# Reordering the opening and the first hand-over of a two-layer adjacency kernel

## The chip, the cores and the metric

One core of one Trainium2 chip runs the whole kernel. The metric is the device time of one execution in microseconds, as a median of runs. The engines are named as in the profile: PE (matrix multiply), PEld (its weight loads), DVE (vector), ACT (activations), POOL and SP (which here mostly issues DMAs).

## The reference: two graph layers on sixteen graphs

For each of 16 graphs, `x` is 1024 x 128 and `adj` is 1024 x 1024 of zeros and ones, all float32. Layer 0 is an attention with gates, layer 1 has four heads (cut to what matters):

```python
h  = x @ Ww.T + Wb
e  = (h @ A) @ h.T ;  e = e + e.T
att = softmax(where(adj > 0, e, 0), axis=1) * adj
hp = relu(att @ h)
ic, fc, oc = (sigmoid(hp @ w_u + x @ w_x) for each gate)
x  = layernorm(x + oc * tanh(ic * hp + fc * x))
# layer 1, per head
h1 = x @ conv_w[hd] + conv_b[hd]
Ah = tanh(adj * (h1 @ attn_w[hd] @ h1.T))
x  = layernorm(x + relu(relu(mean_hd(relu(Ah @ h1))) + x))
```

## The kernel before: tiles, stages and the order of the work

A graph is cut into eight blocks of 128 rows (`NB`), or two halves of 512 columns. The kernel is a software pipeline over graphs: while layer 1 of graph b runs (32 steps of one head and one block, `layer1_step`, lines 589 to 622), pieces of layer 0 of graph b+1 are put between its matmuls. Every engine executes its own instructions strictly in the order in which the program issues them, and that order is written by hand: `run(first, "...")` takes named pieces of layer 0 of graph 0, `run(second, "...")` those of graph 1. For graph 0 there is no layer 1 to hide behind, so lines 674 to 716 order the opening alone.

The pieces have one-letter names: `L` loads a block of adj, `E` makes a 0/1 mask of it (line 383), `Q` projects a half of `qT` (line 242), `H`/`h` multiply and add a third of `h` (lines 327, 331), `S` is a block row of scores: a matmul at line 346 and an ACT eviction at line 349 into the big tile `R`. Scores are symmetric, so only the upper triangle is multiplied. `T` transposes the rest: for graph 0 on PE (line 364) with an ACT copy (line 365), for later graphs through DRAM (`hop`, lines 263 to 276). `A` masks a block row in place and takes its maximum on DVE (line 390), then ACT takes the exponential (line 397). `B` multiplies by adj on DVE (line 406), scales a block of `h` on ACT (line 411) and accumulates the block before on PE (line 422). `R` and `P` give hp and its transpose (lines 431, 441, 442), `G` the gates and `u = fc * x` on POOL (lines 466 to 478), `I` adds `ic * hp` and takes tanh (lines 504, 508), `O`, `V`, `N` end in the layer norm (lines 515, 217 to 222, 233). After that `turn_first_x1` transposes the new x (lines 569, 570), `head_uT` multiplies it by a head's weights (line 242, `pT_u`) and layer 1 of graph 0 can start.

Ahead of this the weights are prepared (lines 66 to 164): `a_sym = A + A.T`, `s_ww = a_sym @ Ww` (`p_s`), `q_w = Ww.T @ s_ww` (`p_q`), bias vectors (`p_c`, `p_sb`, `p_bsb`), the rows of the three gates and of Wb turned to columns (`p_rows`). `keep_at_work` (line 136) issues transposes of the identity whose results nobody reads. `join_weights` (line 176) joins the layer-1 weights in four parts, each `next(join)` one of them: `p_last`; `cw` on DVE and `p_cwT`; `p_caT`; `p_m`.

PSUM has four tiles of 128 x 512 (tag `sc`) for everything but the accumulators. A matmul into one waits until the instruction that read its former content is done.

Of the kernel before, what the change touches and what calls it, by code (L numbers as in the profile page):

```python
# [19 lines left out]
P = 128  # L20
# [4 lines left out]
def two_layer_adjacency_kernel(  # L25
# [37 lines left out]


    ident = consts.tile([P, P], F32, name="ident")
    make_identity(nc, ident)
# [8 lines left out]

    rows_x = sb.tile([4, P], F32, tag="s1", name="rows_x", bufs=4)
    for g, w in enumerate((Wb, wi_x, wf_x, wo_x)):
        nc.scalar.dma_start(rows_x[g : g + 1], w.rearrange("(o d) -> o d", o=1))
    rows_u = sb.tile([3, P], F32, tag="turn", name="rows_u", bufs=2)
    for g, w in enumerate((wi_u, wf_u, wo_u)):  # L80
        nc.gpsimd.dma_start(rows_u[g : g + 1], w.rearrange("(o d) -> o d", o=1))

# [15 lines left out]

    def load_late_weights():
        nc.sync.dma_start(cw_in[0:1], conv_b.rearrange("(o h) d -> o h d", o=1))  # L100
        nc.sync.dma_start(cw_in[1:P], conv_w[:, 0 : D - 1, :].rearrange("h f d -> f h d"))
        nc.sync.dma_start(cw_last, conv_w[:, D - 1 : D, :].rearrange("h f d -> f h d"))
        nc.sync.dma_start(aw, attn_w.rearrange("h i j -> i h j"))
        for g, w in enumerate((wi_u, wf_u, wo_u)):
            nc.sync.dma_start(wu_b[:, g, :], w.partition_broadcast(P))
# [20 lines left out]
    q_w = consts.tile([P, P], F32, name="q_w")  # L126
    c_col = consts.tile([P, 1], F32, name="c_col")
    sb_col = consts.tile([P, 1], F32, name="sb_col")
    b_wide = sb.tile([P, P], F32, tag="uT1", name="b_wide")
    ones = sb.tile([1, P], F32, tag="u", name="ones", bufs=1)  # L130
    nc.gpsimd.memset(ones, 1.0)

# [3 lines left out]
    def keep_at_work(n):  # L136
        for _ in range(n):
            nc.tensor.transpose(idle[:, :P], ident, ident)

    keep_at_work(8)  # L140
    pa, pb = small("p_a"), small("p_ww")
    nc.tensor.transpose(pa[:, :P], a_in, ident)
    nc.tensor.transpose(pb[:, :P], ww_in, ident)
    nc.vector.tensor_add(a_sym, pa[:, :P], a_in)
    nc.scalar.copy(wwT, pb[:, :P])
    keep_at_work(2)
    pa, pb = small("p_s"), small("p_rows")
    nc.tensor.matmul(pa[:, :P], a_sym, ww_in, start=True, stop=True)
    nc.vector.tensor_copy(s_ww, pa[:, :P])
    nc.tensor.matmul(pb[:, :4], rows_x, ident[:4, :4], start=True, stop=True)  # L150
    nc.tensor.matmul(pb[:, P : 2 * P], ones, rows_x[0:1, :], start=True, stop=True)
    nc.vector.tensor_copy(wb_col, pb[:, 0:1])
    nc.vector.tensor_copy(gate_x, pb[:, 1:4])
    nc.scalar.copy(wb_row[:, :D], pb[:, P : 2 * P])
    nc.gpsimd.tensor_copy(b_wide, wb_col.to_broadcast([P, P]))
    pa, pc = small("p_q"), small("p_c")
    nc.tensor.matmul(pa[:, :P], s_ww, ww_in, start=True, stop=True)
    nc.vector.tensor_copy(q_w, pa[:, :P])
    nc.tensor.matmul(pc[:, :1], s_ww, wb_col, start=True, stop=True)
    nc.vector.tensor_copy(c_col, pc[:, :1])  # L160
    nc.vector.tensor_copy(wwT_g[:, G - 1 : G], pc[:, :1])
    pd = small("p_sb")
    nc.tensor.matmul(pd[:, :1], a_sym, wb_col, start=True, stop=True)
    nc.vector.tensor_copy(sb_col, pd[:, :1])

    def finish_weights():
        pt = small("p_bsb")
        nc.tensor.matmul(pt[:, :1], b_wide, sb_col, start=True, stop=True)
        nc.vector.tensor_copy(wb_row[:, G - 1 : G], pt[:, :1])

    def turn_rows_u():
# [119 lines left out]
    def layer0(b):  # L291
# [22 lines left out]
        def project_q(q):  # L314
            if q == 0:
                t["qT"] = sb.tile([P, N], F32, tag="qT0", name=f"qT0_{b}", bufs=1)
            project_T(t["qT"], q_w, t["xT"], c_col, f"q0_{b}", [q])

# [19 lines left out]

        def score(j):
            if j == 0:  # L340

                t["R"] = sb.tile([P, NB, NB, P], F32, tag="R", name=f"R_{b}", bufs=1)
            for q in range(j // BH, NH):
                ps = ps_sc.tile([P, 512], F32, tag="sc", name=f"sc0_{b}_{j}_{q}")
                lo, at = max(q * 512, j * P), (q + 1) * 512
                nc.tensor.matmul(  # L346
                    ps[:, : at - lo], t["qT"][:, ts(j, P)], t["xT"][:, lo:at], start=True, stop=True
                )
                nc.scalar.activation(  # L349
                    t["R"][:, lo // P : at // P, j, :],  # L350
                    ps[:, : at - lo].rearrange("p (k d) -> p k d", d=P),
                    AF.Identity, bias=t["h"][:, j, G - 1 : G],
                )

        def turn_score(j):
# [3 lines left out]
            if b == 0:  # L359
                for l0 in range(0, L, 4):  # L360
                    ls = range(j + 1 + l0, min(j + 5 + l0, NB))
# [12 lines left out]
            hop(R[:, j, j + 1 :, :], sq[:, :w], f"turn0_{b}_{j}")  # L374

        def find_edges(j):

            if b == 0:
                m = sb.tile([P, N], BF16, tag="h1", name=f"edge_{b}_{j}", bufs=NB + 1)
            else:  # L380
                m = sb.tile([P, N], U8, tag="edge", name=f"edge_{b}_{j}")
            engine = nc.vector if b == 0 and j not in (1, 4, 6) else nc.gpsimd
            engine.tensor_scalar(m, adj_t[b, j], 0.0, None, ALU.is_gt)  # L383
# [86 lines left out]
        def forget():  # L470
            t["u"] = sb.tile([P, NB, D], F32, tag="u", name=f"u0_{b}", bufs=1)
            t["x1"] = sb.tile([P, NB, D + 1], F32, tag="x1", name=f"x1_{b}")
            for ks in PARTS:
                nc.gpsimd.tensor_mul(
                    t["u"][:, ks], t["x"][:, ks],
                    t["gate"][:, ks, 1:2].to_broadcast([P, ks.stop - ks.start, D]),
                )
            nc.gpsimd.memset(t["x1"][:, :, 0:1], 1.0)
# [51 lines left out]
        if b == 0:  # L530
            pieces.update(P=lambda: rows_hp(GROUPS), G=gates)
        else:
# [11 lines left out]
        for j in range(NB):  # L544
# [4 lines left out]
            if j + 1 < NB:  # L549
                pieces[f"T{j}"] = partial(turn_score, j)  # L550
        return pieces

# [124 lines left out]
    run(second, "L0 L1 L2 L3 L4 L5 L6 L7")  # L677
    run(first, "E0 E1 E4 E6 Q0")
    finish_weights()
    run(first, "H0 h0 E2 S0 Q1 T0 S1 A0 E3 T1 S2 A1 H1 h1 B0 T2 S3 A2 E5 B1 H2 h2 T3 S4 A3 E7 B2")  # L680
    turn_rows_u()
# [3 lines left out]
    run(second, "H0")  # L685
    run(first, "B6 B7")
    run(second, "h0")
    run(first, "R")
    run(second, "H1 h1")
    run(first, "P")  # L690
    run(second, "H2 h2")
    next(join)
    run(first, "G")
    run(second, "S0")
    run(first, "I0")
    next(join)
    run(first, "I1")
    run(second, "S1")
    next(join)
    run(first, "O0 V0 O1")  # L700
    run(second, "S2")
    next(join, None)
    run(first, "N0")
    run(second, "S3")
    turn_first_x1(x1_t[0], 0)
# [7 lines left out]
    land()  # L713
    run(second, "T2 E0 Q1")
    rows(0, range(BH, NB))
# [105 lines left out]
```

## Time and profile before

| | us |
|---|---|
| median of 4 runs | 2421.18 (2420.8 to 2421.99) |
| the profiled execution | 2421.18 |
| its span in the profile | 2419.4 |
| PE busy | 2404.4 (99% of the span) |
| DVE busy | 1553.2 (64%) |
| ACT busy | 1074.2 (44%) |
| POOL busy | 613.6 (25%) |

The span is the time from the first to the last instruction of the profile; the rest of the execution's time, 1.78 us, lies around it. Times in rows are microseconds from the start of the span, durations too unless marked ns. In a row of a timeline the first number is the start, the second the duration, then engine, line, operation, what it writes and reads, and how many instructions are merged in the row. In the chain of waits each row is a start, a duration, and the work that carried the chain then.

### The profile page before, as it was taken

The page shows a single profiled execution, that of the slowest core. Times are in us where ns is not written, and L with a number is a line of the kernel's source. Part 1 is how long each engine was busy: PE and PEld are TensorE (multiplying, and loading weights), DVE is VectorE, ACT ScalarE, POOL GpSimd, SP SyncE. Part 2 cuts the span into 40 slices and gives each one's busy share as a digit, 9 for nine tenths or more (in the row PEclk, how much of TensorE's full clock was granted, in tenths as well). Part 3 has the DMA queues.
Part 4 walks back from the last instruction along what each step waited for, and adds up shares of the span by engine and source line. Part 5 has one row for each costly group of instructions (what it writes and reads, how often), then busy time and mean ns, then how long its engine had stood idle before and what let it go on. Part 6 is the DMA issues. An engine that isn't in the chain of part 4 may idle for free.

```text
span 2419.4 us, 20189 instructions
## 1 busy us (share of the span) xinstructions
PE 2404.4 (99%) x5966; PEld 1097.7 (45%) x5966; DVE 1553.2 (64%) x3274; ACT 1074.2 (44%) x1502; POOL 613.6 (25%) x382
## 2 busy tenths in 40 slices
PE   8999999999999999999999999999999999999998
PEld 5444444444444444444444444444444444444444
DVE  6656576666666666676666665666666576666554
ACT  5544444443444544444444454444544344443333
POOL 2314031241312413124131331312214132141000
PEclk9999999999999999999999999999999999999999
DMA  4334151341514415143242432425234252341010
GB/s 179 79 69 114 44 136 48 83 126 34 139 37 95 114 48 126 44 104 96 57 118 52 111 81 66 109 61 122 61 72 112 53 127 56 79 117 31 18 26 9
DMA packets 473308, 196.71 MB, mean 81 GB/s; under 512 B 414442, under 2 KB 439278, under 8 KB 473199
## 3 DMA queue, kind: packets, MB, share of 16 engines
q1 hardware_dynamic: 454519, 128.70, 22.5%
q0 software_dynamic: 18384, 66.59, 9.1%
q8 instruction: 47, 0.77, 0.1%
q14 instruction: 62, 0.51, 0.1%
q10 hardware_dynamic: 296, 0.13, 0.0%
HBM read 135.86 MB, written 59.51 MB: 81 GB/s over the span
## 4 chain that ended last, share of the span: by engine, by line
PE 98%; DVE 1%; ACT 0%; DMA 0%; issue 0%; POOL 0%; POOLq 0%; DVEq 0%; ACTq 0%
PE sc L606 36%; PE acc L612 36%; PE acc L422 9%; PE sc L346 5%; PE pR L577 5%; PE pT_u L242 5%; PE pR_h L327 1%; PE pT_q L242 1%; DVE R L390 0%; DVE R L406 0%; PE acc_q L635 0%; DMA a_in<-in_L_gnn_A_dram 0%; DMA rows_x<-in_L_gnn_wo_x_dram 0%; ACT R L397 0%; PE pt L441 0%
## 5 line engine op out<-in xcount | busy, mean ns | idle before, releaser
L607 DVE TENSOR_TENSOR s<-sc,adj 128x512 f32<-128x512 f32 x1008 | 685.4, 688 | 715.8 <-PE sc L606 694.7
L608 ACT ACTIVATE s<-s 128x1024 f32<-128x1024 f32 x504 | 533.1, 1058 | 1032.4 <-DVE s L607 1026.5
L606 PE MATMUL sc<-uT,x1T 128*128 128x512 f32 x2048 | 962.4, 592 | 0.0
L612 PE MATMUL acc<-s,h 128*128 128x512 f32 x2016 | 947.3, 592 | 0.0
L612 PEld LDWEIGHTS acc<-s,h 128*128 128x128 f32 x2016 | 380.6, 190 | 484.6 <-issue 474.2
L606 PEld LDWEIGHTS sc<-uT,x1T 128*128 128x128 f32 x2048 | 387.1, 190 | 469.7 <-issue 403.9
L383 POOL TENSOR_SCALAR edge<-adj 128x1024 uint8<-128x1024 f32 (+1 forms) x123 | 341.0, 2773 | 321.5 <-DVE top_None L390 317.4
L222 POOL TENSOR_TENSOR rs<-rs,mhalf 128x8 f32<-128x8 f32 (+3 forms) x36 | 55.1, 1530 | 948.9 <-DVE rs L221 948.9
L422 PE MATMUL acc<-R,hz 128*128 128x512 f32 x512 | 240.9, 593 | 1.2 <-ACT hz L411 1.1
L397 ACT ACTIVATE R<-R,nmax 128x1024 f32<-128x1024 f32 x128 | 146.9, 1148 | 73.8 <-DVE nmax L395 72.5
L390 DVE CUSTOM_DVE_ANT_0 R<-R,edge 128x1024 f32<-128x1024 f32 (+1 forms) x128 | 154.4, 1206 | 2.7 <-PE turn L364 2.2
L406 DVE TENSOR_TENSOR R<-R,adj 128x1024 f32<-128x1024 f32 x127 | 154.5, 1216 | 0.0
L422 PEld LDWEIGHTS acc<-R,hz 128*128 128x128 f32 x512 | 96.8, 190 | 123.5 <-issue 115.3
L346 PE MATMUL sc<-xT,qT 128*128 128x512 f32 (+3 forms) x384 | 146.7, 491 | 0.0
L349 ACT ACTIVATE R<-sc,h 128x512 f32<-128x512 f32 (+1 forms) x192 | 110.9, 579 | 54.3 <-PE sc L346 49.2
L454 POOL TENSOR_TENSOR x1T<-hp,wu_b 128x1024 f32<-128x1024 f32 x45 | 106.4, 2365 | 105.2 <-DVE hws L460 63.7
L242 PE MATMUL pT_u<-x1T,ms 128*128 128x512 f32 x256 | 120.6, 593 | 0.8 <-ACT x1T L570 0.8
L577 PE MATMUL pR<-cw,x1T 128*128 128x512 f32 x256 | 117.6, 598 | 0.0
L346 PEld LDWEIGHTS sc<-xT,qT 128*128 128x128 f32 x384 | 70.2, 192 | 69.7 <-issue 61.1
L308 POOL DMA_DIRECT2D adj<-in_adjT_dram x112 | 65.5, 585 | 92.6 <-DVE s L607 92.6
L630 DVE SCALAR_TENSOR_TENSOR sum<-acc,sum 128x512 f32<-128x512 f32 x95 | 61.3, 687 | 42.1 <-PE acc L612 42.1
L580 ACT COPY h<-pR 128x512 f32<-128x512 f32 x128 | 72.3, 592 | 28.1 <-PE pR L577 26.4
(139 smaller groups left out, 1137.0 us busy)
## 6 DMA issues: line engine op xcount, KB each, us to landing
adj<-in_adjT_dram POOLq DMA_DIRECT2D x112, 512.0 KB, 4.0
adj<-in_adjT_dram SPq DMA_DIRECT2D x16, 512.0 KB, 7.2
x<-in_x_dram SPq DMA_DIRECT2D x16, 512.0 KB, 5.3
xT<-in_xT_dram SPq DMA_DIRECT2D x15, 512.0 KB, 10.9
dram_hp<-turn_hp SPq DMA_DIRECT2D x15, 512.0 KB, 2.6
hp<-dram_hp SPq DMA_DIRECT2D x60, 128.0 KB, 3.8
dram_x<-turn_x SPq DMA_DIRECT2D x15, 512.0 KB, 3.0
x1T<-dram_x SPq DMA_DIRECT2D x60, 128.0 KB, 5.7
```

The lines of the kernel that those rows point to most:

```text
L242: nc.tensor.matmul(ps, w, src[:, ts(q, 512)], start=True, stop=True)
L346: nc.tensor.matmul(ps[:, : at - lo], t["qT"][:, ts(j, P)], t["xT"][:, lo:at], start=True, stop=True)
L383: engine.tensor_scalar(m, adj_t[b, j], 0.0, None, ALU.is_gt)
L390: nc.vector.tensor_tensor_reduce(s[:, ks], s[:, ks], t["edge", j][:, ks], 1.0, nmax, ALU.mult, ALU.max, top)
L397: nc.scalar.activation(s, s, AF.Exp, bias=nmax, accum_out=t["z", j])
L406: nc.vector.tensor_mul(s, s, adj)
L422: nc.tensor.matmul(t["acc"][:, ts(q, 512)], t["hz", j], t["R"][:, ts(q, BH), j, :], start=(j == 0), stop=(j == NB - 1),)
L577: nc.tensor.matmul(ps, x1T_t[b][:, ts(k, P)], cw.rearrange("p h d -> p (h d)"), start=True, stop=True)
L606: nc.tensor.matmul(ps, x1T[:, ts(m, P)], uT[:, ts(q, 512)], start=True, stop=True)
L607: nc.vector.tensor_mul(s[:, ts(q, 512)], ps, adj[:, ts(q, 512)])
L608: nc.scalar.activation(s, s, AF.Tanh)
L612: nc.tensor.matmul(acc[:, ts(q, 512)], h1[:, ts(hd, D)], s[:, ts(q, 512)], start=(m == 0), stop=(m == NB - 1),)
```

## The change: what moves, and the diff

- The filler matmuls of `keep_at_work` multiply a tile of zeros (`warm`, set by DVE) instead of transposing the identity: 7 and 2 where there were 8 and 2, and one more behind `p_c` and one behind the first projection.
- Wb gets a tile of its own, `wb_in`, still loaded on ACT's queue. The three gate rows of x move to POOL's DMA queue, where the three of u were; those of u move to SP's queue, ahead of the layer-1 weights. `ones` is set by DVE.
- `p_q` comes ahead of the bias vectors; the gate rows are turned only in `finish_weights`, together with `p_bsb`. `c_col` is a view of a column that was written anyway.
- The first half of `qT` is evicted in two pieces of 128 and 384 columns.
- The first turned scores (`T0`) are made by halves between the halves of `S1`, and DVE copies them to their place (`t0`) after the first mask, where ACT did it before.
- `Q1` goes from ahead of `T0` to behind `B0`. On DVE the masks 0 to 4 and 7 are made, on POOL 5 and 6 (before: POOL 1, 4, 6).
- `p_last` goes ahead of the last accumulations of graph 0, and `cw` with `p_cwT` ahead of the gates; `p_caT` and `p_m` each come one place sooner. `H2`, `S1`, `S2`, `S3`, `h2` and `Q1` of graph 1 are put around them in another order.
- `u` of graph 0 is made by three engines: blocks 0 and 1 on DVE, 2 to 5 on ACT, 6 and 7 on POOL.

```diff
+    warm = sb.tile([P, N], F32, tag="sum", name="warm", bufs=1)
+    nc.vector.memset(warm[:, :P], 0.0)
+    ones = sb.tile([1, P], F32, tag="u", name="ones", bufs=1)
+    nc.vector.memset(ones, 1.0)
...
-    rows_x = sb.tile([4, P], F32, tag="s1", name="rows_x", bufs=4)
-    for g, w in enumerate((Wb, wi_x, wf_x, wo_x)):
-        nc.scalar.dma_start(rows_x[g : g + 1], w.rearrange("(o d) -> o d", o=1))
+    wb_in = sb.tile([1, P], F32, tag="x1T", name="wb_in")
+    nc.scalar.dma_start(wb_in, Wb.rearrange("(o d) -> o d", o=1))
+    rows_x = sb.tile([3, P], F32, tag="s1", name="rows_x", bufs=4)
+    for g, w in enumerate((wi_x, wf_x, wo_x)):
+        nc.gpsimd.dma_start(rows_x[g : g + 1], w.rearrange("(o d) -> o d", o=1))
     rows_u = sb.tile([3, P], F32, tag="turn", name="rows_u", bufs=2)
-    for g, w in enumerate((wi_u, wf_u, wo_u)):
-        nc.gpsimd.dma_start(rows_u[g : g + 1], w.rearrange("(o d) -> o d", o=1))
...
     def load_late_weights():
+        for g, w in enumerate((wi_u, wf_u, wo_u)):
+            nc.sync.dma_start(rows_u[g : g + 1], w.rearrange("(o d) -> o d", o=1))
...
     def keep_at_work(n):
         for _ in range(n):
-            nc.tensor.transpose(idle[:, :P], ident, ident)
-
-    keep_at_work(8)
+            nc.tensor.matmul(idle[:, :P], warm[:, :P], warm[:, :P], start=True, stop=True)
+
+    keep_at_work(7)
...
+    nc.tensor.matmul(pb[:, :P], a_sym, ww_in, start=True, stop=True)
+    nc.vector.tensor_copy(s_ww, pb[:, :P])
+    pc, pw = small("p_b"), small("p_ww")
+    nc.tensor.transpose(pw[:, :P], ww_in, ident)
+    nc.tensor.matmul(pc[:, P : P + 1], wb_in, ones[:, 0:1], start=True, stop=True)
+    nc.tensor.matmul(pc[:, :P], ones, wb_in, start=True, stop=True)
...
+    pq, pc = small("p_q"), small("p_c")
+    nc.tensor.matmul(pq[:, :P], s_ww, ww_in, start=True, stop=True)
+    nc.vector.tensor_copy(q_w, pq[:, :P])
+    nc.tensor.matmul(pc[:, 0:1], s_ww, wb_col, start=True, stop=True)
+    nc.tensor.matmul(pc[:, 1:2], a_sym, wb_col, start=True, stop=True)
+    nc.vector.tensor_copy(c_col, pc[:, 0:1])
+    nc.vector.tensor_copy(sb_col, pc[:, 1:2])
+    keep_at_work(1)
 
     def finish_weights():
         pt = small("p_bsb")
         nc.tensor.matmul(pt[:, :1], b_wide, sb_col, start=True, stop=True)
+        nc.tensor.matmul(pt[:, 1:4], rows_x, ident[:3, :3], start=True, stop=True)
         nc.vector.tensor_copy(wb_row[:, G - 1 : G], pt[:, :1])
+        nc.vector.tensor_copy(gate_x, pt[:, 1:4])
...
+            for at, to in ((0, P), (P, 512)):
+                nc.scalar.activation(
+                    t["qT"][:, at:to], ps[:, at:to], AF.Identity, bias=c_col
+                )
...
+        def turn_first_score(half):
+
+            ls = range(max(half * BH, 1), (half + 1) * BH)
+            t["turned", half] = ps = small(f"turn0_0_{half}")
+            for i, l in enumerate(ls):
+                nc.tensor.transpose(ps[:, ts(i, P)], t["R"][:, l, 0, :], ident)
+
+        def place_first_score():
+            for half in range(NH):
+                ls = range(max(half * BH, 1), (half + 1) * BH)
+                nc.vector.tensor_copy(
+                    t["R"][:, 0, ls[0] : ls[-1] + 1, :],
+                    t["turned", half][:, : len(ls) * P].rearrange("p (l d) -> p l d", d=P),
+                )
...
-            engine = nc.vector if b == 0 and j not in (1, 4, 6) else nc.gpsimd
+            engine = nc.vector if b == 0 and j not in (5, 6) else nc.gpsimd
...
-            for ks in PARTS:
-                nc.gpsimd.tensor_mul(
-                    t["u"][:, ks], t["x"][:, ks],
-                    t["gate"][:, ks, 1:2].to_broadcast([P, ks.stop - ks.start, D]),
-                )
+            if b:
+                shared = slice(0, NB)
+            else:
+                shared = slice(NB - 2, NB)
+                for k in range(NB - 2):
+                    mul = nc.vector.tensor_scalar_mul if k < 2 else nc.scalar.mul
+                    mul(t["u"][:, k, :], t["x"][:, k, :], t["gate"][:, k, 1:2])
+            nc.gpsimd.tensor_mul(
+                t["u"][:, shared], t["x"][:, shared],
+                t["gate"][:, shared, 1:2].to_broadcast([P, shared.stop - shared.start, D]),
+            )
...
-    run(first, "E0 E1 E4 E6 Q0")
+    run(first, "E0 Q0")
+    keep_at_work(1)
     finish_weights()
-    run(first, "H0 h0 E2 S0 Q1 T0 S1 A0 E3 T1 S2 A1 H1 h1 B0 T2 S3 A2 E5 B1 H2 h2 T3 S4 A3 E7 B2")
+    run(first, "H0 h0 E1 E2 E5 E6 S0 T0.0 S1.0 T0.1 S1.1 A0 t0 E3 T1 S2 A1 E4 H1 h1 B0 Q1 T2 S3 A2")
+    run(first, "B1 H2 h2 T3 S4 A3 E7 B2")
     turn_rows_u()
     run(first, "T4 S5 A4 B3 T5 S6 A5 B4 T6 S7 A6")
     run(second, "Q0")
     run(first, "B5 A7")
     run(second, "H0")
-    run(first, "B6 B7")
-    run(second, "h0")
-    run(first, "R")
-    run(second, "H1 h1")
+    next(join)
+    run(first, "B6 B7 R")
+    run(second, "h0 H1")
     run(first, "P")
-    run(second, "H2 h2")
+    run(second, "h1")
     next(join)
     run(first, "G")
     run(second, "S0")
+    next(join)
     run(first, "I0")
-    next(join)
+    run(second, "H2 S1")
     run(first, "I1")
-    run(second, "S1")
-    next(join)
+    next(join, None)
+    run(second, "S2")
     run(first, "O0 V0 O1")
-    run(second, "S2")
-    next(join, None)
+    run(second, "h2 S3 Q1")
     run(first, "N0")
-    run(second, "S3")
```

## The prediction, made before the changed kernel ran

> **What bounds the kernel now.** I read the page's busy shares first (PE 99%), then busy time by stretches, to see where the 15 us without PE lie.
>
> ```profile
> core 0: us, PE busy (x) PEld busy (x) DVE busy (x) ACT busy (x) POOL busy (x), PEclk, DMA share, GB/s
> 0.00:5.00 5.00, 2.63 (x10) 1.94 (x11) 0.29 (x1) 0.73 (x1) 3.16 (x15) 1.00 0.61 223
> 5.00:10.00 5.00, 4.29 (x16) 3.55 (x16) 1.49 (x8) 1.08 (x3) 1.67 (x2) 1.00 0.84 306
> 25.00:30.00 5.00, 5.00 (x22) 2.79 (x22) 4.93 (x10) 4.24 (x8) 0.00 (x0) 1.00 0.20 58
> 50.00:60.00 10.00, 7.61 (x27) 4.34 (x26) 8.58 (x35) 5.42 (x10) 3.19 (x4) 0.83 0.00 0
> 70.00:80.00 10.00, 10.00 (x25) 4.56 (x24) 5.64 (x11) 6.77 (x11) 2.77 (x1) 1.00 0.70 129
> ```
>
> From 63 us to 2402 us PE is full, and the change leaves its work there alone. So only lost PE time ahead of the first layer-1 scores (line 606, 73.10 us) can be won. Its size: all matmuls ahead of them, fillers left out, at the full-speed rates of this trace (0.86 us per 128x512 product, 0.22 per 128x128, 0.11 per transpose) come to 52.4 us. Lost: 20.7 us, and the tail is not touched. By the same count, 10.0 us are lost by the first scores (12.89), 14.6 by the transpose of hp (46.00), 20.6 by `pT_u` (63.12). The chain of waits names the causes:
>
> ```profile
> 4.01 2.80 DMA rows_x<-in_L_gnn_wo_x_dram
> 9.44 1.92 PE pT_q L242 x2
> 11.57 1.53 PE pR_h L327 x6
> 15.04 0.86 PE pT_q L242 x2
> 39.74 5.58 PE acc L422 x12
> 50.22 1.05 POOL u L474
> 51.37 0.95 issue
> 53.20 0.61 DVE cw L181
> 54.52 2.98 PE sc L346 x4
> ```
>
> The third gate row holds up the weights; the first `pT_q` takes 1.92 us, the same product later 0.86: PE runs at half speed at first although the clock column says 1.00 there. Behind 50 us DVE waits for POOL's `u`, PE for DVE's `cw`, and then the clock itself falls (0.83). In between, DVE is full: the row 25 to 30, and masks from 16.39 on.
>
> ```profile
> 14.22 0.69 ACT L349 ACTIVATE R<-sc,h 128x512 f32<-128x512 f32 x1 [2.15 <-PE sc L346]
> 16.39 1.10 DVE L390 CUSTOM_DVE_ANT_0 R<-R,edge 128x512 f32<-128x512 f32 x1 [1.63 <-PE turn L364]
> 19.78 1.23 DVE L390 CUSTOM_DVE_ANT_0 R<-R,edge 128x1024 f32<-128x1024 f32 x1 [0.56 <-PE turn L364]
> ```
>
> **Part 1, the weights (0 to 14 us).** The fillers are two passes each: 0.43 us at half speed. Seven fill PE from about 1.0 (DVE's memset replaces the wait for the identity, 1.34) to 4.0, when A lands (3.99): no loss. Two more end at 5.1, where `p_s` can start instead of 5.50. Before, `p_q` then waited for the third gate row (6.81) and 1.2 us of `p_rows`; now only for `p_ww` and the Wb pair, about 1.15 us at half speed: 6.8 instead of 8.07. Wb is issued at 1.64, and must land by 5.7; its neighbours took 2.8 to 3.6 us, so it lands near 5. The filler behind `p_c` is on the path: 0.2 to 0.4 us. `pT_q` starts at 8.6 at half speed, 7.7 at full, instead of 9.30. From there to the first eviction of scores were 4.92 us (9.30 to 14.22). To be added: a filler, the turned gate rows, two DVE copies of 0.15 us and two hand-overs that `pR_h` now waits for, together 0.75 us at full speed, 1.1 at half. To be taken off at full speed: 1.06 (`pT_q`), 0.7 to 0.8 (`pR_h`, `p_bsb`). First eviction: 11.5 us with the full clock from about 6.6 on, 13.25 with it from about 10, 14.6 if it comes as late as before. The two pieces of `qT` gain nothing: the scores are queued behind `pR_h`, which is later.
>
> Which of the three? Durations put the change of speed at 13.4 us before; in the epilogue the clock falls at 54.34 and returns at 57.80. The Trainium skill, "TensorE: Matmul & The Clock Gate", Part 1, says that PE is at half speed until one window of about 3.4 us was busy, that the windows run free, and that the cold count varies by run and should not be fitted; its Part 4 says that transposes do not count as busy. 57.80 minus thirteen windows is 13.4: the rows agree. The windows then end at 3.2, 6.6, 10.0, 13.4. Before, the one that ended at 10.0 was busy by 94% of the rows but only half by columns, and did not raise the clock. Now I count 3.0 of 3.4 us by columns in the one that ends at 6.6, and 2.8 in the next. By the rule the first suffices, by the row alone (half is too little) either could. Whether zeros count no row shows; in the later window real products make up 70%. The same rule speaks against exactness: the phase may differ per run, worth some 1 us.
>
> **Part 2, first scores to hp.** The first mask came 2.17 us behind the first eviction; with `T0` by halves it waits for half of the row: 0.69 + 0.33 + hand-over, 1.1 us. Masks 1 and 2 of the edges (0.69 each on DVE) run while DVE waits for these scores. But `t0` puts two PSUM copies, about 0.57 and 0.69 us by lines 331 and 181, on DVE between the first mask and the second, so the second mask comes 4.15 us behind the first instead of 3.39. Mask 2 of rows: 1.1 + 4.15 = 5.25 behind the eviction instead of 5.56. Then `E4` fills the 0.4 us wait ahead of `h1`, and `E5` no longer stands ahead of `B1`; against it `Q1`'s eviction (0.69) now delays ACT behind `B0`, and with it the third exponential, by 0.6. DVE's chain at `B2` (28.93 before) stands at -2.2, -0.3 or +1.05 us for the three clocks: sums of 11.5, 13.25, 14.6 against 14.22, the 0.31 above, and the rest nearly even. From there DVE, and then the last accumulations (39.74), only shift. `p_last` (0.86) fits PE's wait of 0.77 us for line 411: 0.1 lost.
>
> **Part 3, the epilogue.** From the transpose of hp to `pT_u` were 17.1 us. `cw` falls in DVE's idle time ahead of the gates, so the 2.4 us wait of `p_cwT` goes. What is late next is ACT: behind the gates it now has four products of `u` (0.37 each, overlapped 1.3 us), and behind them in its queue two evictions (1.45), `caT` (0.58) and the first tanh. Set out from hp at 45.2 in the case of the middle: gates done 49.1, ACT's `u` 50.45, evictions 51.9, `caT` 52.45, tanh 53.1, `O0` and statistics 55.55, the power on POOL 56.7, `h2` and `N0` 58.35, transposes and x1T 59.4. That is 14.25 us: 2.9 less. `Q1` (0.86) is in it, which came later before: 3.7. PE waits in it for ACT to free PSUM, about 0.8 us at a time. Behind it the second half's `N1` makes PE wait 0.4. DVE's `u` and `I` may be blocked by POOL's remaining 0.55 us, as they were for 0.95; they end 1 us ahead of ACT's queue, so nothing. Sum: 3.2 us won.
>
> **Queues.** On POOL the gate rows of x take the place of those of u, whose landings were 3.9 to 4.6 us: by 6.6, needed at 9. The skill, "SBUF — State Buffer", section "SBUF: two separate sides", warns that DMAs from this queue wait for descriptors while DVE holds the shared port; DVE's memsets are over before the first of them at 1.49, so I go by the row. On SP three small DMAs (0.25 to 0.5 us each) precede the layer-1 weights; `cw_last` was issued by 27.84, so it comes by 30 to 32, and is needed at 38. Graph 1's DRAM hops start with `N1`, only 0.5 us sooner, while PE comes 3 to 5 us sooner: the fifth mask (91.01 before) falls together with the landing of the hop issued until 84.76; DVE has 2.8 us idle behind it, so I take nothing.
>
> **Cases.** The profiled execution took 2421.18 us, as the median.
> - Full clock two windows sooner: 2.2 + 3.2 - 0.1, some 5.3: 2415.8. Chance 0.42.
> - One window sooner: 0.3 + 3.2: 2417.7. Chance 0.28. For it: zeros may not count.
> - Clock as before: -1.05 + 3.2: 2419.0. Chance 0.18; also the case where the fillers do not do what they are for.
> - Slower: in the epilogue PE now waits repeatedly for ACT's `u` and evictions. If two windows there fall below what holds the clock, each costs up to 1.7 us (half of 3.4), and with the opening as in the last case the sum is 2422.4. It decides once PE is idle for two thirds of a window, as between 51.5 and 53.9 before; I count pauses of under 1 us. Chance 0.12, with costs unknown to me in it.
>
> 0.2% is 4.84 us, about what a measurement can tell from no change: the bound is 2416.3. Beyond it I put 0.35 of the first case and 0.03 of the second: faster 0.38. Slower than 2426.0: 0.04. Within: 0.58. The likeliest single case is the first, its own range 2414.8 to 2416.8; the range below leaves out 0.1 at each end.
>
> **What would show it.** Right: the first product of `pT_q` at 0.43 us per instruction; the first masks at 12.6 (14.4 in the second case); `t0` 1.2 us on DVE; accumulations of graph 0 from 37.5; no wait of PE for `cw`; ACT without a pause from 49 to 55; line 606's first at 67.8 instead of 73.10, and the same spacing from there to the end. Wrong: `p_b` waiting for Wb, `t0` over 1.5 us, a granted clock of 0.5 between 50 and 60, PE waiting for masks at 87, or `p_last` for its DMA.

## The result, and the profile after

The changed kernel takes 2418.45 us as a median of 42 runs (2416.22 to 2420.29), beside 2421.21 (2420.33 to 2422.26, 60 runs) for the kernel before: ratio 0.9988, 95% interval 0.9984 to 0.9993. That is 2.8 us less, inside the range and inside 0.2%, and 2.6 us short of the likeliest case (2415.8). It lies between the prediction's second and third cases (2417.7 and 2419.0), but neither of them happened: the clock rose as soon as in the first case, and time was lost elsewhere. That the number fell where most of the chance had been put is luck. The profiled execution took 2417.44 us with a span of 2415.4: 1 us under the median. The changed kernel's runs lie further apart than those of before; how far that is understood is said at the end of the account below.

Lines are numbered here as in the changed kernel: L142 fillers, L250 eviction of `qT`, L357 scores and L360 their eviction, L416 mask, L432 product with adj, L437 `hz`, L448 weighted accumulation, L643 first scores of layer 1. Where an experiment adds or takes out lines, its numbers are shifted by as many.

Busy time by stretches, after:

```profile
0.00:5.00 5.00, 3.96 (x18) 3.94 (x19) 0.58 (x3) 1.28 (x1) 3.03 (x14) 1.00 0.62 204
20.00:25.00 5.00, 3.27 (x7) 1.35 (x6) 3.28 (x7) 3.44 (x7) 0.29 (x1) 0.74 0.07 20
25.00:30.00 5.00, 5.00 (x19) 2.53 (x17) 3.05 (x7) 2.85 (x6) 0.00 (x0) 0.92 0.07 20
50.00:60.00 10.00, 9.15 (x41) 5.49 (x39) 9.31 (x44) 8.76 (x18) 1.87 (x3) 1.00 0.01 2
```

The row from 20 to 25 before:

```profile
20.00:25.00 5.00, 4.55 (x21) 2.52 (x20) 4.52 (x10) 4.43 (x12) 0.00 (x0) 1.00 0.07 21
```

PE's busy time (second number) rose from 2.63 to 3.96 in the first stretch and from 7.61 to 9.15 in the epilogue, whose clock is now 1.00 instead of 0.83. But a new hole has opened from 20 to 25: PE 3.27 where it was 4.55, with a fallen clock, and DVE, which was full from 25 to 30, works 3.05 of 5 us there.

PE's timeline at the start and at the hole (start, duration, and in brackets the idle time before and what ended it). The first row is of before:

```profile
5.50 0.64 PE L148 MATMUL p_s<-ww_in,a_sym 128*128 128x128 f32 x2
```

```profile
5.25 0.44 PE L149 MATMUL p_s<-ww_in,a_sym 128*128 128x128 f32 x2
21.86 1.55 PE L357 MATMUL sc<-xT,qT 128*128 128x512 f32 x2 [1.73 <-ACT qT L250]
23.20 3.19 PE L448 MATMUL acc<-R,hz 128*128 128x512 f32 x4
27.98 1.88 PE L448 MATMUL acc<-R,hz 128*128 128x512 f32 x4
40.46 5.42 PE L448 MATMUL acc<-R,hz 128*128 128x512 f32 x12
```

`p_s` took 0.64 us before and takes 0.44 now: the clock is up at 5.3 us. At 20.1 PE stops for 1.73 us, and the four accumulations behind that take 3.19 us; the next four take 1.88. The granted clock (third number from the end) shows the fall at 22.4 us and the return at 25.8:

```profile
22.25:22.50 0.25, 0.25 (x2) 0.11 (x1) 0.25 (x1) 0.25 (x3) 0.00 (x0) 0.84 0.07 20
22.50:22.75 0.25, 0.25 (x2) 0.19 (x1) 0.25 (x1) 0.22 (x1) 0.00 (x0) 0.50 0.07 20
25.75:26.00 0.25, 0.25 (x2) 0.23 (x1) 0.00 (x0) 0.00 (x0) 0.00 (x0) 0.83 0.07 18
```

ACT's and DVE's timelines say who was late:

```profile
20.83 0.40 ACT L437 ACTIVATE hz<-h,rz 128x128 f32<-128x128 f32 x1 [1.50 <-DVE rz L433]
21.14 0.67 ACT L250 ACTIVATE qT<-pT_q,wwT_g 128x512 f32<-128x512 f32 x1
```

```profile
12.86 0.69 DVE L416 CUSTOM_DVE_ANT_0 R<-R,edge 128x512 f32<-128x512 f32 x1 [0.47 <-PE turn L392]
16.45 1.22 DVE L416 CUSTOM_DVE_ANT_0 R<-R,edge 128x1024 f32<-128x1024 f32 x1
26.88 0.43 DVE L342 TENSOR_TENSOR h<-pR_h,wb_row 128x264 f32<-128x264 f32 x1 [3.57 <-PE pR_h L338]
29.41 1.22 DVE L432 TENSOR_TENSOR R<-R,adj 128x1024 f32<-128x1024 f32 x1
```

`Q1`'s product is done in PSUM at 18.9, and ACT is idle from 19.3 to 20.8. But ACT takes its work in order, and `Q1` stands behind `B0`, whose `hz` waits for DVE. So the eviction of `qT` starts at 21.14; until it is done its PSUM tile is taken. The four tiles go round: behind `Q1` come two for the turned row 2, one for the first scores of row 3, and then `Q1`'s again. So the second scores of row 3 wait for it, with all of PE behind them. The lead over before shrinks accordingly: at the second mask it was 3.3 us (16.45 against 19.78), at `B2` (29.41 against 28.93) it is gone.

### The profile page after: what moved, and what is told of

Its sections match the earlier page's. It is cut to its first block, busy times and chain, and to the rows that moved or that the text cites. A ratio compares the mean times of both kernels' runs of the same rounds, so it can differ in the third digit from the quotient of the medians.

```text
span 2415.4 us, 20226 instructions
## 1 busy us (share of the span) xinstructions
PE 2403.8 (100%) x5980; PEld 1097.9 (45%) x5980; DVE 1555.2 (64%) x3280; ACT 1074.3 (44%) x1505; POOL 611.5 (25%) x379
## 4 chain that ended last, share of the span: by engine, by line
PE 99%; DVE 1%; ACT 0%; issue 0%; POOLq 0%; DVEq 0%; ACTq 0%
PE sc L643 36%; PE acc L649 36%; PE acc L448 9%; PE sc L357 5%; PE pR L614 5%; PE pT_u L246 5%; PE pR_h L338 1%; PE pT_q L246 1%; PE idle L142 0%; DVE R L416 0%; PE acc_q L672 0%; DVE R L432 0%; DVE edge L409 0%; PE pt L467 0%; PE pt L606 0%
## 5 line engine op out<-in xcount | busy, mean ns | idle before, releaser
L643 PE MATMUL sc<-uT,x1T 128*128 128x512 f32 x2048 | 962.4, 592 | 0.0
L643 PEld LDWEIGHTS sc<-uT,x1T 128*128 128x128 f32 x2048 | 387.0, 190 | 469.8 <-issue 403.9
L448 PE MATMUL acc<-R,hz 128*128 128x512 f32 x512 | 241.9, 595 | 0.1
L416 DVE CUSTOM_DVE_ANT_0 R<-R,edge 128x1024 f32<-128x1024 f32 (+1 forms) x128 | 154.2, 1204 | 0.7 <-PE turn L392 0.5
L432 DVE TENSOR_TENSOR R<-R,adj 128x1024 f32<-128x1024 f32 x127 | 154.5, 1216 | 0.0
L448 PEld LDWEIGHTS acc<-R,hz 128*128 128x128 f32 x512 | 97.5, 191 | 123.1 <-issue 116.8
L357 PE MATMUL sc<-xT,qT 128*128 128x512 f32 (+3 forms) x384 | 145.8, 488 | 2.1 <-ACT qT L250 1.7
L360 ACT ACTIVATE R<-sc,h 128x512 f32<-128x512 f32 (+1 forms) x192 | 110.9, 580 | 53.2 <-PE sc L357 47.9
L357 PEld LDWEIGHTS sc<-xT,qT 128*128 128x128 f32 x384 | 69.6, 190 | 71.5 <-issue 59.6
```

The costliest lines, as they stand in the source:

```text
L357: nc.tensor.matmul(ps[:, : at - lo], t["qT"][:, ts(j, P)], t["xT"][:, lo:at], start=True, stop=True)
L416: nc.vector.tensor_tensor_reduce(s[:, ks], s[:, ks], t["edge", j][:, ks], 1.0, nmax, ALU.mult, ALU.max, top)
L432: nc.vector.tensor_mul(s, s, adj)
L448: nc.tensor.matmul(t["acc"][:, ts(q, 512)], t["hz", j], t["R"][:, ts(q, BH), j, :], start=(j == 0), stop=(j == NB - 1),)
L643: nc.tensor.matmul(ps, x1T[:, ts(m, P)], uT[:, ts(q, 512)], start=True, stop=True)
```

## The experiments

All ran beside the kernel before. Times are medians, with range and number of runs.

| kernel | us | ratio to before, 95% interval |
|---|---|---|
| q1_first | 2415.42 (2414.08 to 2419.23, 9) | 0.9977 (0.9967 to 0.9987) |
| fill_turned | 2418.16 (2416.22 to 2420.64, 11) | 0.9988 (0.9979 to 0.9997) |
| end_alone | 2417.86 (2416.84 to 2418.53, 11) | 0.9985 (0.9976 to 0.9993) |
| start_alone | 2420.98 (2418.37 to 2423.83, 11) | 0.9998 (0.9989 to 1.0006) |
| before_fill | 2420.32 (2418.39 to 2421.91, 11) | 0.9997 (0.9988 to 1.0005) |
| few_fill | 2420.01 (2419.55 to 2420.56, 11) | 0.9996 (0.9987 to 1.0005) |
| q1_edges_dve | 2414.24 (2413.73 to 2419.26, 10) | 0.9973 (0.9964 to 0.9983) |
| q1_u_pool | 2416.51 (2415.91 to 2419.77, 11) | 0.9981 (0.9973 to 0.9990) |
| fill_pause | 2416.76 (2415.67 to 2421.51, 11) | 0.9985 (0.9976 to 0.9994) |
| edges_t0_act | 2414.18 (2413.70 to 2414.36, 6) | 0.9971 (0.9960 to 0.9983) |
| edges_no_halves | 2414.65 (2414.42 to 2419.74, 8) | 0.9976 (0.9966 to 0.9987) |

The kernel before took 2421.34, 2421.05 and 2420.87 us in the three groups (the first four kernels, the next four, the last three).

**One token moved: q1_first.**

```diff
-... A1 E4 H1 h1 B0 Q1 T2 S3 A2
+... A1 E4 H1 h1 Q1 B0 T2 S3 A2
```

> The changed kernel with one token of the order moved: Q1 stands ahead of B0 instead of behind it. PE's order stays; only ACT now evicts the second half of qT (0.69 us) in its 1.5 us of idle time ahead of hz of group 0, instead of behind it. Theory A (the late eviction of qT makes PE pause 1.73 us at 20.1 to 21.9, and this pause makes the clock fall for one window from about 22.4 to 25.8): the wait of sc for qT is gone, PE does not fall to half speed there, the last weighted accumulations of graph 0 begin at about 37.5 to 38.5 instead of 40.46, the first layer-1 scores at about 67 to 68 instead of 69.33, and the time is 1.5 to 3 us under the changed kernel, 2415.5 to 2417, with less spread. Theory B (DVE's chain of masks and weighted sums sets the pace between 20 and 40 us whatever PE does): the wait goes, but the accumulations stay at 40.5 within 0.3 us, and the time within 0.5 us of the changed kernel's, 2418 to 2419.

Theory A holds: 3.0 us under the changed kernel. Only the smaller spread did not come for all runs: eight of nine lie within 1.7 us, one stands off at 2419.23. ACT and PE of this run:

```profile
20.45 0.67 ACT L250 ACTIVATE qT<-pT_q,wwT_g 128x512 f32<-128x512 f32 x1
21.93 0.40 ACT L437 ACTIVATE hz<-h,rz 128x128 f32<-128x128 f32 x1 [0.81 <-DVE rz L433]
```

```profile
20.74 1.56 PE L357 MATMUL sc<-xT,qT 128*128 128x128 f32 x4 [1.03 <-DVE h L342]
22.38 1.98 PE L448 MATMUL acc<-R,hz 128*128 128x512 f32 x4
38.43 5.42 PE L448 MATMUL acc<-R,hz 128*128 128x512 f32 x12
```

The eviction now stands in ACT's idle time; PE still pauses, for 1.03 us behind DVE, but the clock stays up (1.98 for the accumulations that took 3.19). The last accumulations start at 38.43 instead of 40.46, the first layer-1 scores at 67.29 instead of 69.33. The profiles account for 2.1 of the 3.0 us; the rest is that the changed kernel's profile lies 1 us under its median.

**The wait parted from the clock: fill_pause.** Sixteen more fillers ahead of the waiting scores.

```diff
             for q in range(j // BH, NH) if halves is None else halves:
+                if (b, j, q) == (0, 3, 1):
+                    for _ in range(16):
+                        nc.tensor.transpose(idle[:, :P], ident, ident)
```

> The changed kernel as it is, Q1 behind B0, with 16 transposes of the identity (0.11 us each at full speed, 1.76 us) queued on PE ahead of the scores that wait for the late eviction of qT: the wait stays where it is, only PE is not idle in it. It parts the wait from the clock. Theory A (of the 3 us that Q1's place costs, 1.7 us are the clock's fall in the window behind the pause, the rest the wait): no fall at 22 to 26 us, the last accumulations at 38.5 to 39.3 instead of 40.46, the time 1.2 to 2 us under the changed kernel's, 2416.4 to 2417.2, and the runs closer together than its 2416.2 to 2420.3. Theory B (the late eviction itself delays ACT and DVE by the whole amount, the clock's fall lies beside it): within 0.5 us of the changed kernel's, with the same spread.

The median is where theory A puts it: 1.7 us less than the changed kernel with the wait left in place. The ten closest runs lie within 2.4 us; one stands off at 2421.51. The accumulations started at 40.20, not at 38.5 to 39.3: in the profiled run (2418.06, 1.3 us over its median) the gate rows came 0.68 us late and DVE was slowed for longer than in the profile of the changed kernel (see q1_edges_dve), so the late eviction itself came 1.4 us later. No matmul of PE was slow in it after 5 us (L357 is the filler here, L360 the scores):

```profile
21.40 1.91 PE L357 MATMUL idle<-ident 128*128 128x128 f32 x16
23.30 1.13 PE L360 MATMUL sc<-xT,qT 128*128 128x512 f32 x2
40.20 5.42 PE L451 MATMUL acc<-R,hz 128*128 128x512 f32 x12
```

From these scores to the last accumulations are 16.90 us here, 18.60 in the changed kernel (21.86 to 40.46): 1.70 us, the same as between the medians. So of the 3.0 us that Q1's place costs, some 1.7 are the fallen clock and, by difference, 1.3 the late eviction. The intervals of the table are wider than this split; with each kernel set against the kernel before of its own group it would be 1.4 and 1.8.

**Each end alone: end_alone and start_alone.** In the first, the kernel before gets the order from `B5 A7` on and the three engines' `u`; in the second, the changed kernel gets those of before.

```diff
 # start_alone
-    next(join)
-    run(first, "B6 B7 R")
-    run(second, "h0 H1")
+    run(first, "B6 B7")
+    run(second, "h0")
+    run(first, "R")
+    run(second, "H1 h1")
...
```

> The kernel before with the last part of the change alone: the order from the last weighted accumulations on, cw joined sooner, u of graph 0 by three engines. Theory A (most of what the changed kernel won lies in its epilogue): transpose of hp at 46.0 as before, from there to pT_u 13.4 us instead of 17.1, the clock at 1.00 through the epilogue, the first layer-1 scores at 69.5 instead of 73.10, and the time 3 to 4 us under before, 2417.2 to 2418.2. Theory B (the epilogue's gain hangs on the earlier start and is worth under 2 us by itself): 2419.2 or more.

> The changed kernel with the epilogue of before: its order from the last weighted accumulations on and u of both graphs on POOL. What is left is the start: weights, fillers, turned scores by halves, Q1 behind B0. Theory A (what the start wins up to 12 us is lost again by the pause for the late eviction of qT and the fallen clock): the accumulations at about 40.5 instead of 39.74, the transpose of hp at about 46.5 with p_last (0.86) already done, and the time within 0.7 us of before, 2420.5 to 2421.5. Theory B (the start's gain of 2.2 us arrives at the end): 2419.2 or less.

Theory A holds in both: the epilogue alone wins 3.5 us, the start alone 0.4, with an interval that holds no change. That makes 3.8, and both together gave 2.8; the missing 1 us is no more than the intervals leave open. From the transpose of hp to `pT_u` end_alone takes 13.41 us, the changed kernel 13.37. The changed kernel, then end_alone:

```profile
46.56 2.05 PE L467 MATMUL pt<-ident_g,hpT 128*128 128x131 f32 x16
59.93 1.13 PE L246 MATMUL pT_u<-x1T,ms 128*128 128x512 f32 x2 [0.68 <-ACT x1T L607]
```

```profile
47.17 2.05 PE L441 MATMUL pt<-ident_g,hpT 128*128 128x131 f32 x16
60.58 1.13 PE L242 MATMUL pT_u<-x1T,ms 128*128 128x512 f32 x2 [0.68 <-ACT x1T L576]
```

In end_alone the transpose was expected at 46.0; its profiled run had lost 0.9 us by the first eviction of scores (15.16, before 14.22), in the part that it shares with before. start_alone's profile is of its longest run, 2423.83: PE waits 1.03 us for `h` and then 1.73 for the late `qT`, the granted clock is 0.72 and 0.60 in the two stretches from 20 to 30, and the last accumulations begin at 42.34, later than the 40.5 expected. And with `Q1` ahead of `B0` the start is worth 2.4 us: q1_first against end_alone, 2415.42 against 2417.86.

**What raises the clock: fill_turned, few_fill, before_fill.** Twice as many transposes instead of the zero products; fewer zero products; and the old kernel with more of its old fillers.

```diff
 # fill_turned: the changed kernel
-        for _ in range(n):
-            nc.tensor.matmul(idle[:, :P], warm[:, :P], warm[:, :P], start=True, stop=True)
+        for _ in range(2 * n):
+            nc.tensor.transpose(idle[:, :P], ident, ident)
```

> The changed kernel with each filler product of zeros replaced by two transposes of the identity, the filler of before, so that PE is as long in use by them. Theory A (products of zeros count as work for the clock, transposes do not): the clock comes at about 10 or at 13.4 us instead of 5.3; the first product of pT_q takes 0.86 us for each of its two halves or nearly, the first eviction of scores comes at 13 to 14.6 us instead of 11.41, and the time is 1 to 3 us over the changed kernel's, 2419.5 to 2421.5. Theory B (any instruction in PE's queue counts, and the better start is due to the sooner weights alone): full speed from about 5 to 7 us, the first eviction within 0.4 us of 11.41, the time within 0.5 us of the changed kernel's.

Theory A is refuted. With transposes `pT_q` runs at full speed as well, and the time is the changed kernel's:

```profile
7.52 1.02 PE L324 MATMUL pT_q_first<-xT,q_w 128*128 128x512 f32 x2
```

So it was not the zeros. The Trainium skill, "TensorE: Matmul & The Clock Gate", Part 4, says that transposes do not count as busy in the same way; here the clock was up by 5.4 us with them too (`p_s` at 5.42 took 0.39 us), as with products. The measurement decides: the prediction leaned on that line where it allowed only for columns of products.

```diff
 # few_fill: the changed kernel
-    keep_at_work(7)
+    keep_at_work(3)
```

> The changed kernel with 3 instead of 7 fillers ahead of the transpose of A, so that PE pauses for some 1.5 us from about 2.4 us on. Theory A (one window without a pause is needed): the clock rises one or two windows later, at about 8.7 or more instead of 5.3 us, the first eviction of scores at 12.3 to 13.5 us instead of 11.41; the pause for qT that follows is nearly the same, and the time is 0.5 to 2 us over the changed kernel's, 2419 to 2420.5. Theory B (half a window of work suffices): the rise at 5 to 6 us and the time within 0.5 us of the changed kernel's.

```profile
4.08 0.45 PE L146 MATMUL p_a<-ident,a_in 128*128 128x128 f32 x1 [1.39 <-DMA a_in<-in_L_gnn_A_dram]
13.96 2.76 PE L357 MATMUL sc<-xT,qT 128*128 128x512 f32 x4
25.77 1.12 PE L357 MATMUL sc<-xT,qT 128*128 128x512 f32 x2 [1.61 <-ACT qT L250]
42.68 5.42 PE L448 MATMUL acc<-R,hz 128*128 128x512 f32 x12
```

The pause of 1.39 us ahead of `p_a` keeps the clock down until the first scores are half done (2.76 us for four that take 1.88 at full speed and 3.5 at half): a rise at some 15.8 us, later than theory A's 8.7, and so a first eviction at 15.90 where 12.3 to 13.5 was expected. The time is 1.6 us over the changed kernel, as expected, and all eleven runs lie between 2419.55 and 2420.56. The time agrees for a reason that theory A did not have: the 1.61 us pause for `qT`, from 24.2 to 25.8, did not lower the clock, and from the scores behind it to the last accumulations are 16.91 us, as in fill_pause.

```diff
 # before_fill: the kernel before
-    keep_at_work(8)
+    keep_at_work(12)
...
     nc.tensor.transpose(pa[:, :P], a_in, ident)
+    keep_at_work(2)
```

> The kernel before with nothing changed but the number of its fillers, still transposes of the identity: 12 instead of 8 ahead of the transpose of A, and 2 more between it and that of Ww, so that PE has no pause from 1.34 us to the wait for the gate rows at about 6.1. Theory A (what raises the clock is one window of 3.4 us without a pause, by whatever instruction; before, pauses of 0.72, 0.31 and 0.71 us kept it down): full speed from about 5.4 us instead of 13.4, the first eviction of scores at 11.2 to 12 us instead of 14.22, the last weighted accumulations at 37.5 to 38.5 instead of 39.74, and the time 1 to 2.5 us under before, 2418.7 to 2420.2. Theory B (products of zeros or the sooner weights matter, or the pause for the gate rows undoes it): full speed from 10 us or later, the time within 0.5 us of before.

Here both theories hold in part. In the profiled run, the fastest of the eleven (2418.39, 1.9 us under the median), the clock rises, and falls again:

```profile
6.79 0.38 PE L151 MATMUL p_rows<-ident,rows_x 4*128 4x4 f32 x2 [0.62 <-DMA rows_x<-in_L_gnn_wo_x_dram]
8.54 1.10 PE L243 MATMUL pT_q<-xT,q_w 128*128 128x512 f32 x2
9.62 1.52 PE L328 MATMUL pR_h<-wwT_g,xT 128*128 128x132 f32 x6
13.78 1.02 PE L243 MATMUL pT_q<-xT,q_w 128*128 128x512 f32 x2
```

`p_rows` at 6.79 is at full speed (0.38; before 0.58), six `pR_h` at 9.62 are not (1.52; at full speed 0.91), `pT_q` at 13.78 is again; the granted clock is 0.50 from about 9.8 to 13.2. Between the rise and the fall lie a pause of 0.62 us and, up to 8.5, narrow products: two pairs of 128 columns, the others of 4 and 1. The time is 0.7 us under before, with an interval that holds no change. Fillers that close the pauses were thus enough to raise the clock in this run. In the changed kernel it stays up through the thin matmuls, with two more fillers and sooner weights; what each of these is worth was not tried apart.

**What POOL's masks cost: q1_edges_dve.** The changed kernel makes the masks of edges 5 and 6 on POOL, 3.04 to 3.06 us each in the mean.

```diff
-            engine = nc.vector if b == 0 and j not in (5, 6) else nc.gpsimd
+            engine = nc.vector if b == 0 else nc.gpsimd
...
-... H0 h0 E1 E2 E5 E6 S0 ...   B1 H2 h2 ...   A4 B3 T5 ...
+... H0 h0 E1 E2 S0 ...         B1 E5 H2 h2 ... A4 B3 E6 T5 ...
```

> Q1 ahead of B0 (the run q1_first, 2415.42) and, besides, the masks of edges 5 and 6, which the change left on POOL (3.04 us each there), on DVE (0.68 each): 5 ahead of h2, where DVE waits 0.43 us, and 6 behind B3. In q1_first three operations of DVE took longer while POOL worked on these masks: 1.40 instead of 0.75, 2.06 instead of 1.22, and 1.09 instead of 0.68 us, 1.9 us in all. Theory A (POOL's masks slow DVE down by themselves): these three take 0.75, 1.22 and 0.68 us, DVE gains 1.9 and pays 1.36 less 0.43, the last accumulations come 0.7 to 1 us sooner than 38.43, and the time is 0.5 to 1 us under q1_first, 2414.4 to 2415. Theory B (the long durations have another cause, or DVE pays the whole 1.36 us on its path): within 0.4 us of q1_first or above it.

DVE in q1_first, and then in this run:

```profile
16.96 2.06 DVE L416 CUSTOM_DVE_ANT_0 R<-R,edge 128x1024 f32<-128x1024 f32 x1
19.12 1.09 DVE L409 TENSOR_SCALAR edge<-adj 128x1024 bf16<-128x1024 f32 x1
```

```profile
17.07 1.22 DVE L416 CUSTOM_DVE_ANT_0 R<-R,edge 128x1024 f32<-128x1024 f32 x1
18.40 0.68 DVE L409 TENSOR_SCALAR edge<-adj 128x1024 bf16<-128x1024 f32 x1
```

Theory A, a little more than it promised: the three long operations are gone, the last accumulations start at 37.70 instead of 38.43 although this run's first scores were evicted 0.75 us later (12.03 against 11.28), and the time is 1.2 us under q1_first: nine of ten runs are at or under 2414.80, seven of nine of q1_first at or over 2415.28.

**The three engines' u: q1_u_pool.**

```diff
-                for k in range(NB - 2):
-                    mul = nc.vector.tensor_scalar_mul if k < 2 else nc.scalar.mul
-                    mul(t["u"][:, k, :], t["x"][:, k, :], t["gate"][:, k, 1:2])
+            for ks in PARTS:
+                nc.gpsimd.tensor_mul(t["u"][:, ks], t["x"][:, ks], ...)
```

> Q1 ahead of B0 (q1_first) with u of graph 0 on POOL alone, as before, instead of two parts on DVE, four on ACT and two on POOL; the sooner joining of cw stays. Theory A (the epilogue's gain is cw's: the wait of PE for cw and the fallen clock went with the order, and u by three engines adds little): u is ready about 0.8 us later, but ACT has 1.3 us less to do; transpose of hp to pT_u 13.4 to 14.5 us, clock at 1.00, the time 0 to 1.2 us over q1_first, 2415.4 to 2416.6. Theory B (u by three engines carries half of the gain or more): DVE waits for u as in the kernel before (1.05 us) and is blocked by POOL, PE pauses longer than 2 us and the clock falls again, 15 us or more, 2417 or more.

DVE's first products with `u`, in q1_first and here:

```profile
49.12 2.17 DVE L536 SCALAR_TENSOR_TENSOR u<-hp,gate,u 128x128 f32<-128x128 f32 x8
```

```profile
49.74 2.96 DVE L530 SCALAR_TENSOR_TENSOR u<-hp,gate,u 128x128 f32<-128x128 f32 x8 [1.23 <-POOL u L500]
```

DVE waits 1.23 us and its eight products then take 0.8 us longer, but in the epilogue PE pauses for under 1 us at a time and the clock stays up (1.00 from 50 to 60). Theory A: the three engines give 1.1 us, which leaves some 2.4 of the epilogue's 3.5 to the new order, that of `cw` and of graph 1's pieces together; these were not tried apart.

**The first turned scores: edges_t0_act and edges_no_halves**, both on q1_edges_dve.

```diff
 # edges_t0_act                      # t0: nc.scalar.copy for nc.vector.tensor_copy
-... T0.0 S1.0 T0.1 S1.1 A0 t0 E3
+... T0.0 S1.0 T0.1 t0 S1.1 A0 E3
 # edges_no_halves
-... S0 T0.0 S1.0 T0.1 S1.1 A0 t0 E3
+... S0 T0 S1 A0 E3
```

> Q1 ahead of B0 and all edges of graph 0 on DVE (q1_edges_dve, 2414.24), with the two copies t0 of the turned first scores (1.15 us) on ACT instead of DVE, ahead of the eviction of the second half of the scores of row 1. Theory A (DVE's chain sets the pace from the first mask to the last accumulations, ACT has 0.7 us idle at that place): the second mask at 16.2 instead of 17.07, the last accumulations at 36.9 to 37.2 instead of 37.70, the time 0.5 to 0.9 us under q1_edges_dve, 2413.4 to 2413.8. Theory B (ACT is as late as DVE; what DVE gains it waits for the later eviction): within 0.3 us of it.

> q1_edges_dve with the first scores turned as before: both halves transposed at once behind both scores of row 0, and copied by ACT; the order S0 T0 S1 A0. Theory A (turning by halves brings the first mask 1.1 us sooner, and t0 on DVE gives 0.8 of it back, as the prediction's sum has it, 0.31 us at mask 2): the first mask about 1.1 us later, t0's 1.15 us gone from DVE, the time 0 to 0.5 us over q1_edges_dve, 2414.2 to 2414.8. Theory B (the halves carry a gain of their own of 1 us or more, DVE having been idle before the first mask in any case): 2415.2 or more. Below 2414 neither holds, and the halves are a loss.

The first falls to theory B: 2414.18 against 2414.24. DVE has lost the 1.15 us of copies ahead of the second mask and gained a wait:

```profile
16.47 1.23 DVE L416 CUSTOM_DVE_ANT_0 R<-R,edge 128x1024 f32<-128x1024 f32 x1 [0.80 <-PE turn L375]
```

That transpose waits for ACT's eviction, which the copies delay: ACT was as late as DVE. The second agrees with theory A, at 0.4 us over q1_edges_dve, though the runs of the two overlap: halves gain little, as the sum had it. Its profile is of a run in which the clock rose only at some 17 us, so it can't show the first mask's place.

## Why the prediction was right and wrong, step by step

- **The weights: right, the instant of the rise aside.** First eviction of scores at 11.41 (11.5 forecast), `p_q` at 6.36 (6.8), first mask at 12.86 (12.6), `t0` 1.14 us (1.2). The question left open, whether zeros count, is answered with yes, but transposes count too (fill_turned). What the fillers do is close PE's pauses (few_fill). The windows carried over from before, ending at 6.6 and 10.0, did not fit: the rise came at 5.3. So 11.41 is met in part by luck: a clock that is up 1.3 us sooner brought the eviction only 0.1 us sooner.
- **First scores to hp: the failed step.** The second mask came at 5.04 us behind the first eviction (5.25 forecast, but in parts 1.45 and 3.59 for 1.1 and 4.15), so the start's gain was there. Then the sentence that `Q1`'s eviction "now delays ACT behind `B0`, and with it the third exponential, by 0.6" counted the moved step on ACT's queue alone. Its PSUM tile was not followed to PE, which needs it for the second scores of row 3. In place of 0.6 us the runs show 3.0 (q1_first): 1.3 for the wait, 1.7 for the clock (fill_pause). `B2` was due 2.2 us ahead of before and came 0.5 behind. With the token moved it comes 1.6 ahead (27.37), and with POOL's masks moved too 2.5 (26.43). The kernel with the token moved takes 2415.42 us, and the forecast was 2415.8; that they agree so well is in part luck, for `B2` is still 0.6 short of its forecast and the epilogue won 0.3 more than its own. The sum itself has a gap: 11.5 less 14.22 less 0.31 is -3.0, not -2.2, and in all three cases 0.8 to 1.0 us is taken up by "the rest nearly even" with no term named.
- **The epilogue: right.** 3.2 us forecast, 3.5 measured alone (end_alone), and no wait of PE for `cw` is left. From the transpose of hp to `pT_u` 13.37 us in the changed kernel (14.25 forecast, 17.1 before).
- **The rival on the other side had the right mechanism in the wrong place.** A pause of PE behind ACT, long enough for the clock to fall, worth up to 1.7 us: that happened, at 20 us and not in the epilogue, where no pause is over 0.7. Its threshold, two thirds of a window idle, was too high: 1.73 us, about half of the 3.4 us for which the clock then stayed down, sufficed in the changed kernel.
- **Queues: mostly right.** `cw_last` landed at 29.1 (30 to 32 forecast, needed at 39.4). The gate rows on POOL's queue were to land by 6.6, from the 3.9 to 4.6 us of their neighbours; they took 4.8 to 6.7 us (5.5 to 5.8 in the changed kernel), and in four experiments' profiles `p_bsb` waited 0.33 to 0.68 us for them. In the changed kernel's profile nothing waits.
- **Not in the sum at all:** POOL's two masks slow DVE (0.65 us in the changed kernel's profile, 1.9 in q1_first's, 2.1 in start_alone's). The row of before showed it: the first mask, 128x512, took 1.10 us at 16.39 where the second took 0.75, and POOL was at work on masks from 13.17 to 18.67.

Still open: what makes the changed kernel's 42 times spread over 4 us. Only one of them was profiled. The profiles of the other kernels show three things that differ from run to run: how long POOL slows DVE, which in start_alone put a pause of 1.03 us ahead of the 1.73, with the granted clock at 0.50 from 22.2 to 29.0; how late the gate rows land; and a first rise of the clock at some 17 us (edges_no_halves). Eight of the 42 times lie within 0.15 us of each other, from 2420.15 to 2420.29, where few_fill with its late rise lies (2420.01); that they are late rises too isn't shown. That the fall depends on how the pause lies in a free-running window agrees with few_fill, where 1.61 us did no harm. The skill's Part 1 of the page named above states such a window, of about 3.4 us, but also that the clock falls after a whole idle one, where here a pause of half that length was followed by the fall; no run here fixes the phase.

## What to carry to other kernels

When a step is moved, follow its buffer as well as its engine: an eviction put behind a waiting instruction keeps its PSUM tile, and the matmul that needs that tile holds up all of PE. Judge every pause of PE by what the clock makes of it: here some 1.3 us of late eviction cost 3.0, and filling the pause with idle transposes gave back over half. Then put each part back alone; end_alone, start_alone and one moved token showed that a total of 2.8 us hid 3.5 won in one place, and a start worth 2.4 of which 0.4 or less arrived.

## What the runs showed of the hardware that was not expected

- Transposes of the identity raise the clock as products of zeros do (fill_turned: `pT_q` at full speed from 7.52).
- The clock column shows 1.00 in the first stretch of both kernels, where durations show half speed; only durations tell there.
- The clock fell behind a pause of 1.73 us (the changed kernel, 22.4 to 25.8 us) and of 1.72 (fill_turned); it did not behind 1.03 us (q1_first) or 1.61 us (few_fill). These are single profiles, and no threshold follows: in before_fill it fell with no pause over 0.62 us, among thin matmuls.
- The clock can rise late though PE has no pause ahead of it. The profile of edges_no_halves is of such a run (2419.71; six of its eight runs took 2414.42 to 2414.71): its fillers and `p_a` stand where the changed kernel's do, but `p_s` is at half speed, and all four first scores too.

```profile
5.26 0.63 PE L149 MATMUL p_s<-ww_in,a_sym 128*128 128x128 f32 x2
14.05 3.51 PE L357 MATMUL sc<-xT,qT 128*128 128x512 f32 x4
```

  The single runs at 2419.2 to 2419.8 of q1_first, q1_edges_dve and q1_u_pool lie 3.3 to 5.0 us over their medians, this one 5.1; they were not profiled, so that they are of this kind is a guess.
- A mask on POOL can make a DVE operation that runs beside it longer, by 0.41 to 0.84 us (q1_first), and all three durations were normal once POOL had none (q1_edges_dve). It does not do so each time: the changed kernel's mask at 16.45 took its normal 1.22 us beside one. The Trainium skill, "SBUF — State Buffer", "SBUF: two separate sides", describes a port pair shared by the two engines and held for a whole instruction; the rows agree with waiting of that kind, but show it only for a part of POOL's 3.04 us.
